# Layer norm 1 of batch 2 on x transposed by the host, and Q of unit 8 one block later

## The chip, the cores and the metric

The kernel runs on one core of one Trainium2 chip. The metric is the device time of one execution, in microseconds (us); lower is better. A core has a matrix engine (PE, with its weight loads shown apart as PEld), a vector engine (DVE), an activation engine (ACT), a general engine (POOL) and a sync engine (SP) that in this kernel issues nearly all transfers. Each engine takes its instructions strictly in the order in which the program lists them; semaphores hold an instruction until its inputs are there. DMA transfers issued by SP leave SP's queue in order too, and a transfer that has to wait holds all that stand behind it.

## The reference, cut to what matters

Four batches of a cross-attention block in float32: 512 rows of x, 512 rows of context, width 512, 16 heads of 32.

```python
x = layer_norm(hidden_states, ln1_w, ln1_b)
q = (x @ q_w + q_b).reshape(B, LQ, H, HD).transpose(0, 2, 1, 3)
k = (encoder_hidden_states @ k_w + k_b)...   # and v likewise
scores = jnp.einsum('bhqd,bhkd->bhqk', q, k) * scale
attn = jax.nn.softmax(jnp.where(mask, scores, mask_value), axis=-1)
out = jnp.einsum('bhqk,bhkd->bhqd', attn, v) @ cproj_w + cproj_b   # heads joined first
hidden = out + hidden_states
y = layer_norm(hidden, ln2_w, ln2_b)
y = jax.nn.gelu(y @ fc_w + fc_b, approximate=True) @ proj_w + proj_b
return hidden + y
```

Layer norm 1 is `(x - mu) * rsqrt(var + 1e-5) * w + b` over each row of x. The matrix products that follow contract over the width, so its result is wanted with the width on the partitions, that is transposed.

## The kernel before, in words

**Units, blocks, pairs.** The attention is cut into 16 units `w = 0..15`: batch `w // 4`, a group of four heads. Each unit is run in two halves of 256 query rows, which gives 32 blocks `p = 2w + half`, one after the other. In a block PE computes the scores (L317). DVE adds the mask and finds the row minimum (L323), ACT takes the exponential (L327), DVE transposes 32x32 squares into the tile `tb` (L335), and `copies` (L385 to L399) brings these into a tile with the keys on the partitions: four copies on POOL (L393) and twelve transfers issued by SP (L398). `attend` then multiplies by V (PE, L415) and scales by the reciprocal sums into `oT` (DVE, L420).

**When a pair is attended.** The result of a block is called a pair with the block's number. Around the change, from block 10 on, pair p - 2 is attended at the start of block p, ahead of the scores of that block. Pairs 8, 9, 10, 11 and so on use the one tile `pT`, so the copies and transfers of a pair are issued, in program order, right behind the `attend` of the pair before it. So POOL's copies of pair 10 stand in POOL's order behind all that block 10 gave to POOL, and ahead of what the fills of block 11 give to it; PE needs them for `attend` of pair 10, at the start of block 12.

**The rest of the work is written into the blocks by hand.** `put(p, ...)` lists work for block p as (cost, function). `block` runs the list in three stretches, `fill(0)` to `fill(2)`; in the first two it stops at a budget of 3.4. The costs only decide in which stretch an item is issued; within a block the items keep the list's order. `A(w)` gives the projections K, Q and V of unit w: `prep_k` (PE L255, ACT L257), `prep_q` (PE L267, ACT L268), `prep_v` (PE L278, ACT copy L283, then a bias on POOL, L309). `C(b)` is the output projection of a batch (PE L455, DVE L456). `stat`, `rs`, `norm` and `turns2` are layer norm 2: DVE statistics (L129, L130), POOL L135 to L148 for the reciprocal root (`ln_rs`), the normalisation of the four row tiles (`ln_norm`: ACT L153, for batch 0 the last of the four on DVE L157), and 16 transposes on PE (L166) with weight and bias applied on the way out of PSUM (ACT L171, DVE L169). `fc_sums` forms sums of the first MLP weights on POOL (L597, L600) and stores them (L689, L690); in block 10 it does two pairs of weight blocks. `fc_seven` (PE L646) is the first MLP product.

**Layer norm 1, two ways.** Batches 0 and 2 load x by rows, take statistics, normalise the four tiles and transpose them on PE: 16 transposes (L166) into four PSUM tiles and from there to `xT` with weight and bias. For batch 2 both the normalisation (L153) and the way out of PSUM (L171) are on ACT, since `(1, 2)` is in `BY_ACT` and `NORM_ACT`. Batches 1 and 3 (`BY_ROW`) also load x by rows for the statistics, but load x transposed by the host as well (`load_raw`). The two spreads, `rs` and `-mean*rs`, are turned by DVE (L203), stored to DRAM (`store_rn`, L206) and read back to all partitions (`load_rn`, L213). POOL multiplies and adds them in 128x512 tiles, eight instructions (`ln1_rows`, L218), and ACT applies weight and bias in four (`ln1_affine`, L222).

The blocks that the change edits read so before (line numbers of the profile are those of this kernel):

```python
put(9, c[:1], do(lambda: attend(3, 1)), x2[:2], c[1:2], x2[2:], stat(0, 0), c[2:3], stat(0, 1),
    c[3:], stat(0, 2), x3, stat(0, 3), rs(0))
k, q, v = A(8)
put(10, [k], norm(0, 0, 1), [v], norm(0, 2, 3), do(fc_sums), [q], t2)
k, q, v = A(9)
put(11, [k, v], some(2), pb_(0), mid=do(lambda: y_sums(0)))
```

Here `x2` holds the three parts of layer norm 1 of batch 2 (two of statistics, one of normalisation), `x3` its transposes, `t2` the transposes of layer norm 2 of batch 0, `some(2)` one first MLP product, `pb_(0)` four bias additions on POOL (L426).

Of the kernel before, what the change touches and what calls it, by code (L numbers as in the profile page):

```python
# [12 lines left out]
F32 = mybir.dt.float32  # L13
# [7 lines left out]
P = 128  # L21
B, L, D, H = 4, 512, 512, 16
# [3 lines left out]
ND = D // P  # L26
# [9 lines left out]
IN_G = (1, 3, 5, 7)  # L36
IN_XE = (25, 27, 29, 31)

BY_ROW = ((1, 1), (1, 3))
BY_ACT = ((1, 2),)  # L40
NORM_ACT = BY_ACT + ((2, 0), (2, 1))
MW = 8
WARM = 9
PW = 2 * NT * HG * HD
# [7 lines left out]
def xattn_block(ctx: ExitStack, tc: tile.TileContext, x, rawT, encT, mask, q_w, k_w, v_w, c_w, fc_w, p_w, vecs, rows, out):  # L52
# [3 lines left out]
    def pools(stack, **bufs):  # L56
        return [stack.enter_context(tc.tile_pool(name=n, bufs=k)) for n, k in bufs.items()]

    const, keep, hids, tiles, small = pools(ctx, const=1, keep=1, hids=4, tiles=4, small=4)
# [19 lines left out]
    eT, xT = (xe[:, i * ND * L : (i + 1) * ND * L].rearrange("p (d l) -> p d l", d=ND) for i in range(2))  # L79
# [35 lines left out]
    S = {"gelu": []}  # L115
# [3 lines left out]
    def acc_tile(name):  # L119
        n = count[5]  # L120
        count[5] += len(banks) > 1
        return banks[n // 4 % len(banks)].tile([P, D], F32, tag="acc", name=name)
# [9 lines left out]
    def ln_rs(key):  # L132

        ve = small.tile([P, NT], F32, tag="ve", name=f"ve{key[0]}_{key[1]}")
        nc.gpsimd.tensor_scalar(ve, S["mv", key][:, :, 1], EPS, 1.0, ALU.add, ALU.mult)  # L135
        if key in BY_ROW:
            rs, nm = rn[:, :NT], rn[:, NT : 2 * NT]
# [6 lines left out]
        S["rs", key] = rs  # L144
        if key in NORM_ACT:
            nm = small.tile([P, NT], F32, tag="nm", name=f"nm{key[0]}_{key[1]}")
# [4 lines left out]
    def ln_norm(key, t, dst, src):  # L151
        if key in NORM_ACT and (key, t) != ((2, 0), 3):
            nc.scalar.activation(  # L153
                dst, src, AF.Identity, bias=S["nm", key][:, t : t + 1], scale=S["rs", key][:, t : t + 1]
            )
            return
        nc.vector.tensor_scalar(  # L157
            dst, src, S["mv", key][:, t, 0:1], S["rs", key][:, t : t + 1], ALU.subtract, ALU.mult
        )

    def ln_turn(key, d, xn, dst):

        w, bi = (LN1W, LN1B) if key[0] == 1 else (LN2W, LN2B)
        tp = acc_tile(f"tp{key[0]}_{key[1]}_{d}")
        for t in range(NT):
            nc.tensor.transpose(tp[:, ts(t, P)], xn[t][:, ts(d, P)], ident)  # L166
        wd, bd = vec[:, w + d : w + d + 1], vec[:, bi + d : bi + d + 1]
        if d in (1, 2) and key not in BY_ACT:
            nc.vector.tensor_scalar(dst[:, d, :], tp, wd, bd, ALU.mult, ALU.add)  # L169
        else:  # L170
            nc.scalar.activation(dst[:, d, :], tp, AF.Identity, bias=bd, scale=wd)  # L171
# [23 lines left out]
            ln_rs((1, b))  # L195

    def load_raw(b):
        S["xn", b] = [tiles.tile([P, L], F32, tag="xn", name=f"raw_{b}_{d}") for d in range(ND)]
        for d in range(ND):
            nc.sync.dma_start(out=S["xn", b][d], in_=rawT[b, ts(d, P), :])  # L200

    def store_rn(b):
        nc.vector.transpose(rnT, rn)  # L203
        d = S["rn", b] = dram.tile([2, L], F32, tag=f"rn{b}", name=f"rn{b}")
        for i in range(NI):
            nc.sync.dma_start(  # L206
                out=d.rearrange("a (t i q) -> i (a t) q", i=NI, q=HD)[i], in_=rnT[i * HD : i * HD + 2 * NT, :]
            )

    def load_rn(b):  # L210
        S["rows", b] = [hids.tile([P, L], F32, tag="hid2", bufs=2, name=f"rn_{b}_{i}") for i in range(2)]
        for i in range(2):
            nc.sync.dma_start(out=S["rows", b][i], in_=S["rn", b][i : i + 1, :].broadcast_to([P, L]))  # L213

    def ln1_rows(b, *ds):
        for d in ds:
            for i, op in enumerate((ALU.mult, ALU.add)):
                nc.gpsimd.tensor_tensor(S["xn", b][d], S["xn", b][d], S["rows", b][i], op)  # L218

    def ln1_affine(b):  # L220
        for d in range(ND):
            nc.scalar.activation(  # L222
                xT[:, d, :], S["xn", b][d], AF.Identity,
                bias=vec[:, LN1B + d : LN1B + d + 1], scale=vec[:, LN1W + d : LN1W + d + 1],
            )
# [148 lines left out]
    def target(w, half):  # L374
        pair = 2 * w + half
        return "gt" if pair in IN_G else "xe" if pair in IN_XE else "pT"

    def exchange():

        while waiting and target(*waiting[0]) not in held:  # L380
            w, half = waiting.pop(0)
            held[target(w, half)] = w, half
            copies(w, half)
# [17 lines left out]
    def attend(w, half):  # L401

        b, g = divmod(w, NG)
        if g == 0 and half == 0:
            S["oT", b] = one.tile([P, NG, L], F32, tag="oT", name=f"oT_{b}")
        v, pT = S["v", w], S["pT", w, half]
        av = acc_tile(f"av_{w}_{half}")
        o = S["oT", b][:, g, ts(half, 2 * P)]
        shape, kw = "p (a i q) -> p a i q", dict(a=2, i=NI)
        pv = pT[:, :, :PW].rearrange("p i (a t h q) -> p t h a i q", a=2, t=NT, h=HG)  # L410
        p = [[pv[:, t, h] for h in range(HG)] for t in range(NT)]
        r = pT[:, :, PW:].rearrange("p i (a q) -> p a i q", a=2)
        for t in range(NT):
            for h in range(HG):
                nc.tensor.matmul(  # L415
                    av[ts(h, HD), : 2 * P].rearrange(shape, **kw), v[:, t, ts(h, HD)], p[t][h],
                    start=(t == 0), stop=(t == NT - 1),
                )
        o, a = o.rearrange(shape, **kw), av[:, : 2 * P].rearrange(shape, **kw)
        nc.vector.tensor_tensor(o, a, r, ALU.mult)  # L420
        del held[target(w, half)]
        exchange()
# [173 lines left out]
    def sub(o, x0, x1, engine=None):  # L596
        (engine or nc.vector).tensor_tensor(o, x0, x1, ALU.subtract)  # L597
# [19 lines left out]
    def y_sums(b):  # L617
        y11, y12, y21, y22 = y_blocks(b)
        e = nc.gpsimd if b == SPLIT else nc.vector
        sub(ys[:, 0], y12, y11)  # L620
        sub(ys[:, 1], y22, ys[:, 0])
        sub(y12, y22, y12, e)
        sub(ys[:, 2], y21, ys[:, 1], e)
# [55 lines left out]
    def fc_sums():  # L679

        while count[3] < len(fc_pairs) and count[3] < count[4] + 2:
            b, c = fc_pairs[count[3]]
            if ("fcw", b, 2 * c + 1) not in S:
                return
            x, y = raw_pair(b, c)
            s = wsum[:, count[3] % 2]
            a_sums(x[:, :2], x[:, 2:], y[:, :2], y[:, 2:], s[:, 0], s[:, 1], y[:, :2], s[:, 2], nc.gpsimd)
            if b == 0:
                nc.gpsimd.dma_start(out=sums_dram[c, :, :3], in_=s)  # L689
                nc.gpsimd.dma_start(out=sums_dram[c, :, 3], in_=y[:, :2])  # L690
            S["ws", b, c] = s[:, 0], s[:, 1], y[:, :2], s[:, 2]
            count[3] += 1
# [276 lines left out]
    def do(fn):  # L969
        return [(0.0, fn)]  # L970
# [4 lines left out]
    def A(w):  # L975
        if w >= NW:
            return []
        return [
            (CHAIN, lambda: prep_k(w)),
            (CHAIN, lambda: prep_q(w)),  # L980
            (CHAIN, lambda: prep_v(w)),
        ]
# [69 lines left out]
    def some(n):  # L1052
        taken = []
        while n > 0:
            n -= 1 if mlp[0][0] == CHAIN else 2
            taken.append(mlp.pop(0))
        assert n == 0
        return taken
# [10 lines left out]
    def pb_(b):  # L1069
        return do(lambda: proj_bias(b))  # L1070

    def rs(b):
        return do(lambda: ln_rs((2, b)))

    def stat(b, *ts_):
        return do(lambda: [stat2(b, t) for t in ts_])

    def norm(b, *ts_):
        return do(lambda: [norm2(b, t) for t in ts_])
# [3 lines left out]
    def put(p, *work, before=(), mid=()):  # L1083

        work = [item for part in work for item in part]
        ahead[p], mids[p] = list(before), list(mid)
        fills[p] = work
# [13 lines left out]
    x1, x2, x3, x4 = inputs(2)  # L1101
    k, q, v = A(7)
    c, t2 = C(0), turns2(0)
    put(7, [v6, k], cb(0))
    put(8, x1, [q, v], x4)
    put(9, c[:1], do(lambda: attend(3, 1)), x2[:2], c[1:2], x2[2:], stat(0, 0), c[2:3], stat(0, 1),
        c[3:], stat(0, 2), x3, stat(0, 3), rs(0))
    k, q, v = A(8)
    put(10, [k], norm(0, 0, 1), [v], norm(0, 2, 3), do(fc_sums), [q], t2)
    k, q, v = A(9)  # L1110
    put(11, [k, v], some(2), pb_(0), mid=do(lambda: y_sums(0)))

    x1, x2, x3, x4 = inputs(3)
    put(12, [q], some(2))
    k, q, v = A(10)
# [5 lines left out]
    k, q, v = A(11)  # L1121
    put(16, do(lambda: ln1_rows(3, *range(ND))), [k, q], some(2), h_(1, 0, 1))
    put(17, next_(lambda: ln1_affine(3)), h_(1, 2, 3), x4, cb(1), C(1))
    k, q, v = A(12)
    put(18, [q], some(2), [k])
    k, q, v = A(13)
# [3 lines left out]
    k, q, v = A(14)  # L1130
    t2 = turns2(1)
    put(22, [k, q], norm(1, 0, 1), some(2), norm(1, 2, 3))
    k15, q15, _ = A(15)
    put(23, some(1), [k15], t2, pb_(1), some(1), h_(2, 2, 3, 0, 1))
    c = C(2)
# [32 lines left out]
    c = cproj_last()  # L1168
# [59 lines left out]
```

## Time and profile before

| What | Value |
|---|---|
| median of 3 runs | 763.28 us (763.26 to 763.47) |
| profiled execution, its own time | 766.39 us |
| its span, first to last instruction | 764.3 us |
| mean granted PE clock | 0.997 of full |
| busy: PE, DVE, ACT, POOL | 757.5, 602.0, 337.1, 334.7 us |

The span is the stretch from the first to the last instruction of the profiled execution; 2.1 us of its own time lie around the span, and that own time is 3.1 us over the median of the three runs. In the rows shown below the first number of a timeline or chain row is the start in us from the start of the span, the second the duration; "x16" is a count of instructions merged in one row; a bracket gives the idle time of the engine ahead of the row and what ended it.

### The profile page before, as it was taken

The page shows a single profiled execution, that of the slowest core. Times are in us where ns is not written, and L with a number is a line of the kernel's source. Part 1 is how long each engine was busy: PE and PEld are TensorE (multiplying, and loading weights), DVE is VectorE, ACT ScalarE, POOL GpSimd, SP SyncE. Part 2 cuts the span into 40 slices and gives each one's busy share as a digit, 9 for nine tenths or more (in the row PEclk, how much of TensorE's full clock was granted, in tenths as well). Part 3 has the DMA queues.
Part 4 walks back from the last instruction along what each step waited for, and adds up shares of the span by engine and source line. Part 5 has one row for each costly group of instructions (what it writes and reads, how often), then busy time and mean ns, then how long its engine had stood idle before and what let it go on. Part 6 is the DMA issues. An engine that isn't in the chain of part 4 may idle for free.

```text
span 764.3 us, 12899 instructions
## 1 busy us (share of the span) xinstructions
PE 757.5 (99%) x4370; PEld 518.7 (68%) x4370; DVE 602.0 (79%) x1198; ACT 337.1 (44%) x766; POOL 334.7 (44%) x350
## 2 busy tenths in 40 slices
PE   9999999999989999999999999999999999999998
PEld 6655555566565545475464566458888899988997
DVE  3888999879976777887888889958877886747762
ACT  2566766565863475647753467501202221021200
POOL 1539447368653883443584444532060004303152
PEclk9999999999999999999999999999999999999999
DMA  8999889467796686765666867776724402146001
GB/s 325 341 255 243 204 207 254 111 199 196 214 251 212 194 242 169 184 184 130 167 141 179 212 194 197 171 226 212 270 97 131 163 31 90 36 133 218 1 15 42
DMA packets 60577, 134.59 MB, mean 176 GB/s; under 512 B 11312, under 2 KB 17072, under 8 KB 60384
## 3 DMA queue, kind: packets, MB, share of 16 engines
q1 hardware_dynamic: 58448, 126.73, 58.0%
q0 software_dynamic: 1920, 7.01, 2.8%
q8 instruction: 35, 0.57, 0.3%
q14 instruction: 30, 0.25, 0.1%
q10 hardware_dynamic: 144, 0.02, 0.0%
HBM read 69.23 MB, written 11.02 MB: 105 GB/s over the span
## 4 chain that ended last, share of the span: by engine, by line
PE 98%; SPq 1%; DMA 1%; issue 0%; DVE 0%; POOL 0%; POOLq 0%; DVEq 0%
PE q L646 25%; PE accp L705 11%; PE r L790 8%; PE sc L317 8%; PE av L415 8%; PE acck L255 7%; PE accq L267 7%; PE accc L455 6%; PE accv L278 5%; PE accv L298 3%; PE q1p L844 2%; PE q4p L826 2%; PE tp L166 1%; SPq L398 1%; DMA ptt<-q_w_dram 1%; PE warm L1023 1%
## 5 line engine op out<-in xcount | busy, mean ns | idle before, releaser
L327 ACT ACTIVATE ptt<-ptt,mn 128x512 f32<-128x512 f32 x256 | 181.7, 711 | 147.6 <-DVE mn L323 147.6
L323 DVE CUSTOM_DVE_ANT_0 ptt<-sc,mb 128x512 f32<-128x512 f32 x256 | 160.6, 682 | 20.1 <-PE sc L317 20.0
L335 DVE STREAM_TRANSPOSE tb<-ptt 128x1024 f32<-128x1024 f32 x128 | 153.3, 1217 | 1.0 <-ACT ptt L327 1.0
L393 POOL COPY pT<-tb 32x1088 f32<-32x1088 f32 x96 | 104.5, 1089 | 86.4 <-DMA pbt<-p_w_dram 28.0
L705 PE MATMUL accp<-pbt,gt 128*128 128x512 f32 x192 | 85.3, 596 | 0.0
L646 PE MATMUL q<-yT,gt 128*128 128x256 f32 x320 | 78.9, 380 | 0.0
L667 ACT ACTIVATE ga<-ga,vec 128x512 f32<-128x512 f32 x40 | 26.7, 714 | 93.3 <-DVE ga L600 83.5
L646 PEld LDWEIGHTS q<-yT,gt 128*128 128x128 f32 x320 | 61.0, 191 | 8.1
L705 PEld LDWEIGHTS accp<-pbt,gt 128*128 128x128 f32 x192 | 35.9, 190 | 44.6 <-issue 39.2
L317 PE MATMUL sc<-pbt 32*128 32x512 f32 x512 | 66.1, 621 | 0.0
L646 PE MATMUL q<-ys,gt 128*128 128x256 f32 x240 | 61.6, 380 | 0.0
L255 PE MATMUL acck<-xe,ptt 128*128 128x512 f32 x128 | 58.8, 603 | 0.2 <-issue 0.2
L267 PE MATMUL accq<-xe,ptt 128*128 128x512 f32 (+1 forms) x136 | 58.5, 575 | 0.0
L646 PEld LDWEIGHTS q<-ys,gt 128*128 128x128 f32 x240 | 45.7, 191 | 6.1
L600 DVE TENSOR_TENSOR ga<-q,ga 128x512 f32<-128x512 f32 (+1 forms) x60 | 36.2, 603 | 16.9 <-PE q L646 14.3
L415 PE MATMUL av<-pT,v 128*32 128x256 f32 x768 | 47.3, 387 | 2.0 <-DMA ptt<-q_w_dram 2.0
L327 ACT ACTIVATION_READ_ACCUMULATOR ptt<-ptt,mn 128x1 f32 x256 | 47.8, 187 | 0.0
L267 PEld LDWEIGHTS accq<-xe,ptt 128*128 128x128 f32 x136 | 24.9, 190 | 31.4 <-issue 23.0
L317 PEld LDWEIGHTS sc<-pbt 32*128 32x128 f32 x512 | 27.5, 187 | 26.0 <-issue 17.2
L255 PEld LDWEIGHTS acck<-xe,ptt 128*128 128x128 f32 x128 | 23.6, 192 | 31.2 <-issue 21.9
L455 PE MATMUL accc<-wc,oT 128*128 128x512 f32 x96 | 42.5, 598 | 0.0
L415 PEld LDWEIGHTS av<-pT,v 128*32 128x32 f32 x768 | 23.0, 111 | 26.2 <-issue 10.4
(219 smaller groups left out, 1265.4 us busy)
## 6 DMA issues: line engine op xcount, KB each, us to landing
pT<-tb SPq DMA_DIRECT2D x288, 136.0 KB, 2.4
pbt<-p_w_dram SPq DMA_DIRECT2D x40, 256.0 KB, 3.3
gt<-ws SPq DMA_DIRECT2D x20, 512.0 KB, 3.4
gt<-tb SPq DMA_DIRECT2D x48, 136.0 KB, 3.8
xe<-tb SPq DMA_DIRECT2D x48, 136.0 KB, 2.5
pbt<-fc_w_dram SPq DMA_DIRECT2D x24, 256.0 KB, 4.0
gt<-fc_w_dram SPq DMA_DIRECT2D x20, 256.0 KB, 3.2
ptt<-k_w_dram SPq DMA_DIRECT2D x16, 256.0 KB, 3.7
```

The lines of the kernel that those rows point to most:

```text
L255: nc.tensor.matmul(acc, S["wk", w][:, d, :], eT[:, d, :], start=(d == 0), stop=(d == ND - 1))
L267: nc.tensor.matmul(acc, S["wq", w][:, d, :], xT[:, d, c], start=(d == 0), stop=(d == ND - 1))
L317: nc.tensor.matmul(S["sc", w, qt][h], qT[r, ts(qt, P)], kT[r, :], start=True, stop=True)
L323: nc.vector.tensor_tensor_reduce(out=s, in0=S["sc", w, qt][h], in1=S["mb", w // NG], scale=1.0, scalar=FMAX, op0=ALU.add, op1=ALU.min, acc ...
L327: nc.scalar.activation(s, s, AF.Exp, bias=mn, scale=-1.0, accum_out=S["sums", w][:, qt, h : h + 1])
L335: nc.vector.transpose(tv[:, qt % 2, 2 * k : 2 * k + 2], S["ps", w, qt, k])
L393: nc.gpsimd.tensor_copy(pT[ts(i, HD), i], tb[ts(i, HD), i])
L415: nc.tensor.matmul(av[ts(h, HD), : 2 * P].rearrange(shape, **kw), v[:, t, ts(h, HD)], p[t][h], start=(t == 0), stop=(t == NT - 1),)
L455: nc.tensor.matmul(acc, S["oT", b][:, g, ts(t, P)], wc[:, g, :], start=(g == 0), stop=(g == NG - 1))
L646: nc.tensor.matmul(o, x[:, k], y[:, k], start=(k == 0), stop=(k == 1))
L705: nc.tensor.matmul(acc, gT[q % 2][:, k, ts(t, P)], S["pw", b, q * FQ + k], start=(k == 0), stop=(k == FQ - 1))
L790: nc.tensor.matmul(r, x[:, c], w[:, c], start=(c == 0), stop=(c == NP // 2 - 1))
```

## The change

Batch 2 joins `BY_ROW` and leaves `BY_ACT` (which goes). Its four normalisations on ACT, its 16 transposes on PE and their four ACT instructions go. In their place come, in block 9, four loads of transposed x, straight into `xT`, the turn of the spreads on DVE, four small stores and two loads that spread the rows; in block 10, eight POOL instructions behind the two pairs of `fc_sums`; in block 11, four ACT instructions. Q of unit 8, which reads `xT`, moves from ahead of `t2` in block 10 to the end of block 11, with its bias on ACT (L268) and the load of a later Q weight that it issues. The loads of x by rows and the statistics stay.

```diff
-BY_ROW = ((1, 1), (1, 3))
-BY_ACT = ((1, 2),)
-NORM_ACT = BY_ACT + ((2, 0), (2, 1))
+BY_ROW = ((1, 1), (1, 2), (1, 3))
+NORM_ACT = ((2, 0), (2, 1))
...
-        if d in (1, 2) and key not in BY_ACT:
+        if d in (1, 2):
...
     def load_raw(b):
-        S["xn", b] = [tiles.tile([P, L], F32, tag="xn", name=f"raw_{b}_{d}") for d in range(ND)]
+        S["xn", b] = [
+            xT[:, d, :] if b == 2 else tiles.tile([P, L], F32, tag="xn", name=f"raw_{b}_{d}") for d in range(ND)
+        ]
...
-    put(9, c[:1], do(lambda: attend(3, 1)), x2[:2], c[1:2], x2[2:], stat(0, 0), c[2:3], stat(0, 1),
-        c[3:], stat(0, 2), x3, stat(0, 3), rs(0))
-    k, q, v = A(8)
-    put(10, [k], norm(0, 0, 1), [v], norm(0, 2, 3), do(fc_sums), [q], t2)
+    put(9, c[:1], do(lambda: attend(3, 1)), x2[:2], do(lambda: load_raw(2)), c[1:2], do(lambda: store_rn(2)), stat(0, 0),
+        c[2:3], stat(0, 1), do(lambda: load_rn(2)), c[3:], stat(0, 2, 3), rs(0))
+    k, q8, v = A(8)
+    put(10, [k], norm(0, 0, 1), [v], norm(0, 2, 3), do(lambda: (fc_sums(), ln1_rows(2, *range(ND)))), t2)
     k, q, v = A(9)
-    put(11, [k, v], some(2), pb_(0), mid=do(lambda: y_sums(0)))
+    put(11, [k, v], some(2), pb_(0), do(lambda: ln1_affine(2)), [q8], mid=do(lambda: y_sums(0)))
```

## The prediction

> **What bounds the kernel now.** I read the page first, then the chain of waits around blocks 9 to 12, then ACT and POOL there in order of time.
>
> ```profile
> PE 757.5 (99%) x4370; PEld 518.7 (68%) x4370; DVE 602.0 (79%) x1198; ACT 337.1 (44%) x766; POOL 334.7 (44%) x350
> ...
> PE 98%; SPq 1%; DMA 1%; issue 0%; DVE 0%; POOL 0%; POOLq 0%; DVEq 0%
> ```
>
> PE is busy for 99% of the span and 98% of the chain that ended last lies on it. So PE work that is removed shortens the kernel, one for one, as long as no wait takes its place; and every wait put into PE lengthens it one for one. The chain where the change lies, with start and duration:
>
> ```profile
> 142.58 1.75 PE tp L166 x16
> 144.33 1.86 PE av L415 x32
> 146.19 1.93 PE sc L317 x16
> 148.12 3.63 PE acck L255 x8
> 151.75 3.57 PE accv L278 x32
> 155.33 3.44 PE accq L267 x8
> 158.76 0.22 PE tp L166 x2
> 158.98 0.01 issue
> 158.99 1.75 PE tp L166 x14
> 160.74 1.86 PE av L415 x32
> ...
> 171.74 6.04 PE q L646 x28
> 177.78 1.86 PE av L415 x32
> ```
>
> The reader is to see four things. The first row is the transposes that go. At 146.19 the scores of block 10 begin; K, V and Q of unit 8 follow, and then the transposes of layer norm 2 of batch 0 (158.76). The pair of transposes, then 0.01 us of issue, then fourteen: PE came there at the very moment at which their input did. And `attend` of pair 10 stands at 177.78, after block 11's K, V and first MLP product.
>
> **The transposes removed: -1.75 us.** Sixteen instructions, 1.75 us on the chain, with nothing beside them. Block 10 begins 1.75 us earlier, at 144.44, if nothing else there was waited for; DVE, ACT and POOL of block 10 follow its scores and move with it. The eight ACT instructions that go too are taken at nothing: ACT waits for DVE again in block 10 (the 1.59 us below), so their time is not asked for.
>
> **Q of unit 8 moved: +3.44 us, and nothing back.** Q leaves block 10 and comes back whole in block 11, the same work on PE. But it was the cover of a wait:
>
> ```profile
> 153.95 0.72 ACT L327 ACTIVATE ptt<-ptt,mn 128x512 f32<-128x512 f32 x1 [1.59 <-DVE mn L323]
> ...
> 155.38 0.66 ACT L257 ACTIVATE pbt<-acck,vec 128x512 f32<-128x512 f32 x1
> 155.94 1.51 ACT L153 ACTIVATE xn<-h,nm,rs 128x512 f32<-128x512 f32 x2
> 157.35 0.39 ACT L356 COPY rr<-rsum 128x256 f32<-128x256 f32 x1
> 157.65 0.58 ACT L283 COPY v<-accv 128x512 f32<-128x512 f32 x1
> 158.12 0.82 ACT L153 ACTIVATE xn<-h,nm,rs 128x512 f32<-128x512 f32 x1
> ```
>
> The normalised tiles that the transposes read come from ACT: two at 155.94, the third at 158.12, ready at 158.94, which is where PE's fourteen begin. ACT's own queue sets this: the last exponentials of block 10 wait for DVE, and then K's bias, two normalisations, the reciprocals, V's copy and the third normalisation run without a gap. None of it hangs on Q, whose bias on ACT comes after. So with block 10 1.75 us earlier the third tile is there at 157.19, and the transposes end 1.75 us earlier, at 158.99. PE, without Q, is at them at 158.76 - 1.75 - 3.44 = 153.57, and stands idle for 157.24 - 153.57 - 0.22 = 3.45 us, in two or three pieces. The Q that used to fill this then costs 3.44 us in block 11. By PE and ACT alone, `attend` of pair 10 would be reached at 177.78 - 1.75 + 3.44 = 179.47, that is 1.69 us later than before.
>
> **The eight POOL instructions: they become the last to arrive.** Before `attend` of pair 10, POOL must copy pair 10 into `pT`.
>
> ```profile
> 81.44 4.47 POOL L393 COPY pT<-tb 32x1088 f32<-32x1088 f32 x4
> ...
> 158.37 1.41 POOL L309 TENSOR_TENSOR v<-v,row 128x512 f32<-128x512 f32 x1 [6.91 <-ACT v L283]
> ...
> 169.05 4.69 POOL L393 COPY pT<-tb 32x1088 f32<-32x1088 f32 x4
> ...
> 253.49 10.38 POOL L218 TENSOR_TENSOR raw<-raw,rn 128x512 f32<-128x512 f32 x8
> ```
>
> V's bias starts when ACT has copied V; the weight sums and their stores run to 169.05; the copies end at 173.74, and PE takes them at 177.78: 4.04 us in hand. After the change the eight instructions of `ln1_rows` stand between the stores and the copies, in POOL's order. The same eight for batch 3, in one piece, took 10.38 us. POOL's start hangs on ACT's copy of V in block 10, so it moves with block 10: 158.37 - 1.75 = 156.62. Then 10.68 us to the end of the stores (169.05 - 158.37), 10.38 and 4.69: the copies end at 182.37. PE is there at 179.47 at the earliest, so it waits again, and `attend` of pair 10 begins at about 182.3 instead of 177.78. I take **+4.5 us**. The bounds of this step are narrow, since every part is a measured row: with the four copies at 4.47 us, as at 81.44, it is 0.2 less; if POOL's eight run beside DVE's sums of block 11 and are slowed by them, as an estimate some tenths more.
>
> The sum is not 1.69 + 4.5: the two waits lie one behind the other on PE, and POOL's chain runs past the first. From the start of block 10's scores to `attend` of pair 10 PE needs 31.6 us of work, as before; POOL's chain needs 38 us; and the block starts 1.75 us earlier. That is -1.75 + 38.0 - 31.6, some 4.6, the same figure from the other side. Behind that point nothing gives the time back: K, V and the MLP products follow on PE without gaps, so a shift there lasts to the end.
>
> **What I cost at nothing, and its cover.**
>
> ```profile
> 128.11 9.67 SPq L398 DMA_DIRECT2D pT<-tb  x12
> ...
> 240.51 1.30 SPq L206 DMA_DIRECT2D rn<-rnT  x4
> 242.73 0.82 SPq L213 DMA_DIRECT2D rn<-rn  x2
> ...
> L222 ACT ACTIVATE xe<-raw,vec x8: 797/804/817, 80.0 to 276.6; 128x512 f32<-128x512 f32 x8
> ```
>
> SP is through with pair 8 at 137.78. The loads of transposed x go out behind it (`xT` has no reader left: Q of unit 7 was in block 8), then the stores, which wait for DVE's turn of the spreads (one small instruction amid block 9's statistics), then the two spreading loads. For batch 3 stores to last load took 243.55 - 240.51 = 3.0 us, so SP is held to about 144, and what is queued behind it is the transfers of pair 9. These wait for `attend` of pair 8 anyway, which now ends at 144.4. If SP were held 2 us longer, pair 9 would still be in time for 158.99. The rows themselves are wanted by POOL only at about 167. The four ACT instructions (804 ns each) follow POOL's pairs one by one; the last ends near 178.5, and Q's fourth step on PE comes at about 178.6. Should it be late, it is late inside a stretch in which PE waits for POOL anyway. Behind them on ACT stand only Q's bias and the exponentials of block 12. The load that Q issues is held on SP until Q has run, with pair 11's transfers behind it, and those wait for `attend` of pair 10, which is later still. None of this can gain either.
>
> **The clock after a wait.** The one long wait in the trace of before has a price beside itself:
>
> ```profile
> 218.20:220.17 1.97, 0.00 (x1) 0.03 (x2) 1.76 (x3) 1.94 (x4) 0.00 (x0) 1.00 0.89 275
> 220.17:222.94 2.77, 2.77 (x36) 1.41 (x36) 0.04 (x1) 0.77 (x1) 0.00 (x0) 0.67 1.01 359
> 222.94:225.67 2.73, 2.73 (x17) 1.07 (x17) 1.26 (x4) 0.10 (x1) 2.10 (x2) 0.71 0.94 310
> ```
>
> PE idle for 1.97 us; then the granted clock is 0.67 and 0.71 over the next 5.5 us, and `attend` and the scores take 5.50 us in place of the 1.86 + 1.93 of the other blocks: 1.7 us lost. So the 3.45 us in block 10 will very likely drop the clock too. That costs nothing in the sum: PE would come to pair 10 at 181.2 instead of 179.47, still ahead of POOL at 182.3. What it decides is how long PE then waits: 1.1 us, which I take as too little for a second drop, or 2.8 us if the clock held, which is enough for one by the row above.
>
> The Trainium skill, in "TensorE: Matmul & The Clock Gate", Part 1, has the clock fall back to half only after an idle window of about 3.4 us. This trace contradicts that, with a drop after 1.97 us. By the page no second drop would come in either case, and the time would be that of the forecast; by the row the second drop is a rival.
>
> **The forecast.** Against the profiled execution: 766.39 + 4.5 = 770.9, span 768.8. The runs are compared without a profile, where the median is 763.28; a shift in PE's order is the same in both. Forecast **767.8 us**.
>
> **Rivals.**
> - A second clock drop at pair 10: 4.5 + 1.7 = +6.2, 769.5 us. For it, the drop after 1.97 us; against it, that the first wait will have slowed PE already, so that little is left to wait.
> - The clock drop at 220 goes away, because the later start meets another phase of whatever sets it: +4.5 - 1.7 = +2.8, 766.1 us. Against it: the three runs lie within 0.21 us of each other, so that drop is steady.
> - POOL does not decide: only the wait for the normalised tiles is left, +1.7, or +3.4 with its clock drop, 765.0 to 766.7 us. This needs POOL's chain shorter by 2.9 us (or 1.1): against it stands the 10.38 row.
> - Faster: both waits are absorbed and only the transposes count, -1.75, 761.5 us. It takes ACT, relieved of eight instructions, to bring the third tile 3.45 us earlier, and POOL's copies to end by 176.0 instead of 182.3. It decides from the point where ACT starts K's bias at 151.9, not 153.6. Against it: ACT had 1.59 us idle in block 10, waiting for DVE.
> - No change: the change does less than it says on PE, or part of each of the above cancels; nothing in the profile names such a case.
>
> **How the numbers follow.** Forecast 0.50, second drop 0.20, drop at 220 gone 0.12, POOL not deciding 0.08, faster 0.06, within the bound 0.04. A measurement of this kernel can tell about 0.2% (1.5 us) from no change. The case of +1.7 alone sits at that edge, so 0.01 of it goes to no change: faster 0.06, same 0.05, slower 0.89. The range goes from the wait of block 10 alone (765.0) to the second drop and some tenths of POOL's collisions (769.9).
>
> **What would show it.** Right: in block 10 PE idle for some 3.4 us ahead of the transposes, released by ACT L153; the granted clock below 1 behind it; POOL's copies of pair 10 ending about 38 us after the start of block 10's scores; PE's `attend` waiting for POOL L393; block 12 on shifted by a constant. Wrong: no idle time ahead of the transposes (then ACT was not what they waited for), `attend` of pair 10 released by something else than POOL, or a shift that shrinks after block 12.

## The result, and the profile after

The changed kernel took 771.00 us (median of 4 runs, 768.99 to 774.32) against 763.27 us for the kernel before (4 runs, 761.89 to 763.47): a ratio of 1.0108 [1.0085, 1.0130], slower by about 7.7 us. The forecast was 767.8 us with a range up to 769.9. The direction was right, the size was not: 4.5 us were forecast, and the range ended 1.1 us short.

The profiled execution of the changed kernel has its own time at 774.32 us. From its page: the busy times, and the chain that ended last by engine. Line numbers of the changed kernel are one higher than those of the kernel before from L200 on, and one lower ahead of it.

```profile
PE 760.1 (98%) x4354; PEld 518.4 (67%) x4354; DVE 604.5 (78%) x1199; ACT 334.4 (43%) x762; POOL 345.1 (45%) x358
...
PE 93%; DVE 4%; ACT 1%; issue 1%; DMA 1%; POOL 0%; DVEq 0%; POOLq 0%
```

PE runs 16 instructions fewer and is busy for 2.6 us *longer*. Of the chain 5% have passed from PE to DVE, ACT and issue. POOL, which the forecast had as the last to arrive, has 0%. The waits of PE say who came last instead; columns are total us, times, longest:

```profile
PE accq L268 <- ACT xe L223: 2.7, 1, 2.7
PE tp L165 <- ACT xn L152: 2.6, 3, 1.2
PE av L416 <- DMA ptt<-q_w_dram: 2.6, 1, 2.6
```

The second row is the forecast wait for the normalised tiles. The first is the moved Q itself: it waits for the last of the four new ACT instructions. The third is the transfer ahead of pair 13, which the profile of before had too (218 to 220) and which is spoken of below. PE in order of time:

```profile
154.83 0.33 PE L165 MATMUL tp<-ident,xn 128*128 128x128 f32 x1 [1.11 <-ACT xn L152]
155.54 0.33 PE L165 MATMUL tp<-ident,xn 128*128 128x128 f32 x1 [0.38 <-ACT xn L152]
157.03 3.25 PE L165 MATMUL tp<-ident,xn 128*128 128x128 f32 x14 [1.16 <-ACT xn L152]
...
179.99 5.40 PE L268 MATMUL accq<-xe,ptt 128*128 128x512 f32 x8 [2.67 <-ACT xe L223]
185.32 1.93 PE L416 MATMUL av<-pT,v 128*32 128x256 f32 x32
...
228.43 3.59 PE L416 MATMUL av<-pT,v 128*32 128x256 f32 x32 [2.64 <-DMA ptt<-q_w_dram]
```

Both waits have a slow stretch behind them. The fourteen transposes take 3.25 us instead of 1.75, and Q takes 5.40 instead of 3.44 (in the chain, whose rows do not overlap; in a timeline an undisturbed Q has 3.60 to 3.70 us). The windows over these stretches have the granted clock in the last column but two:

```profile
157.00:159.00 2.00, 1.97 (x9) 1.98 (x10) 0.39 (x1) 0.78 (x1) 1.92 (x3) 0.50 0.32 117
159.00:161.00 2.00, 2.00 (x22) 1.38 (x25) 1.23 (x2) 0.69 (x1) 1.73 (x3) 0.68 0.00 0
...
180.00:183.00 3.00, 3.00 (x5) 1.37 (x6) 1.81 (x3) 2.05 (x3) 2.84 (x4) 0.63 0.00 0
183.00:186.00 3.00, 3.00 (x19) 1.14 (x21) 0.00 (x0) 0.57 (x1) 3.00 (x3) 0.80 0.02 5
```

So the terms up to `attend` of pair 10 are: transposes -1.75; slow transposes 3.25 - 1.75 = +1.50; Q +3.44; the wait ahead of Q +2.67; slow Q 5.40 - 3.44 = +1.96. The sum is +7.82. The trace has the same: from `attend` of pair 7, where nothing is changed yet (130.15 before, 129.93 after), to `attend` of pair 10 (177.71 before, 185.32 after) it is 47.56 us before and 55.39 after, +7.83 us. Pair 14 and those behind it stand a constant 8.28 to 8.29 us later than before: 7.83, less the 0.22 by which pair 7 was earlier, and 0.67 more at pair 13, where the wait is longer than before.

Why ACT was late with Q's input is told by the chain of waits between block 11's scores and Q:

```profile
165.77 0.62 DVE ys L598
...
166.48 2.13 DVE ys L598
168.60 1.68 DVE yT L598
170.28 1.67 DVE ys L598
171.96 0.60 DVE ptt L324
...
176.09 1.52 ACT ptt L328 x4
...
178.47 0.48 ACT v L284
...
179.23 0.72 ACT xe L223
...
179.99 5.40 PE accq L268 x8
```

The first four rows are `y_sums(0)`, sums of the transposed activations that DVE forms amid block 11's mask-and-minimum work (L597 before, L598 after; neither is edited). Behind them wait the other four row minima, behind these ACT's exponentials, and behind those, in ACT's queue, V's copy among others and at last the new `ln1_affine` (L223). DVE in order of time, before:

```profile
166.14 0.92 DVE L597 TENSOR_TENSOR ys<-yT 128x512 f32<-128x512 f32 x1
167.17 1.03 DVE L597 TENSOR_TENSOR ys<-yT,ys 128x512 f32<-128x512 f32 x1
168.12 0.68 DVE L597 TENSOR_TENSOR yT<-yT 128x512 f32<-128x512 f32 x1
168.73 0.68 DVE L597 TENSOR_TENSOR ys<-yT,ys 128x512 f32<-128x512 f32 x1
```

and in the changed kernel, DVE and then POOL:

```profile
165.69 0.69 DVE L598 TENSOR_TENSOR ys<-yT 128x512 f32<-128x512 f32 x1
166.48 2.13 DVE L598 TENSOR_TENSOR ys<-yT,ys 128x512 f32<-128x512 f32 x1
168.53 1.75 DVE L598 TENSOR_TENSOR yT<-yT 128x512 f32<-128x512 f32 x1
170.21 1.75 DVE L598 TENSOR_TENSOR ys<-yT,ys 128x512 f32<-128x512 f32 x1
```

```profile
166.77 11.49 POOL L219 TENSOR_TENSOR xe<-xe,rn 128x512 f32<-128x512 f32 x8
178.20 4.47 POOL L394 COPY pT<-tb 32x1088 f32<-32x1088 f32 x4
```

The four sums took 3.31 us before and 6.32 after. The three long ones lie beside POOL's eight row instructions. POOL's copies end at 182.67; that is close to the forecast 182.37, but PE comes only at 185.32, so they hold nobody.

### The profile page after: what moved, and what is told of

Read it like the earlier page. It is cut to its first block, busy times and chain, and to the rows that moved or that the text cites. A ratio compares the mean times of both kernels' runs of the same rounds, so it can differ in the third digit from the quotient of the medians.

```text
span 772.5 us, 12886 instructions
## 1 busy us (share of the span) xinstructions
PE 760.1 (98%) x4354; PEld 518.4 (67%) x4354; DVE 604.5 (78%) x1199; ACT 334.4 (43%) x762; POOL 345.1 (45%) x358
## 4 chain that ended last, share of the span: by engine, by line
PE 93%; DVE 4%; ACT 1%; issue 1%; DMA 1%; POOL 0%; DVEq 0%; POOLq 0%
PE q L647 24%; PE accp L706 11%; PE r L791 8%; PE sc L318 8%; PE accq L268 8%; PE av L416 7%; PE acck L256 6%; PE accv L279 4%; PE accc L456 4%; PE accv L299 3%; PE q1p L845 2%; PE q4p L827 2%; DVE ptt L324 1%; PE tp L165 1%; DVE tb L336 1%
## 5 line engine op out<-in xcount | busy, mean ns | idle before, releaser
L268 PE MATMUL accq<-xe,ptt 128*128 128x512 f32 (+1 forms) x136 | 60.2, 589 | 2.7 <-ACT xe L223 2.7
L268 PEld LDWEIGHTS accq<-xe,ptt 128*128 128x128 f32 x136 | 25.5, 194 | 35.5 <-issue 23.7
```

What stands on the lines that cost most here:

```text
L268: nc.tensor.matmul(acc, S["wq", w][:, d, :], xT[:, d, c], start=(d == 0), stop=(d == ND - 1))
```

## The experiments

Theory: the wait for the normalised tiles slows the clock and delays block 11; DVE's four sums then fall beside the POOL row instructions and take twice as long; through ACT's queue that makes Q wait, and the clock drops again. The rival is the forecast: POOL's copies of pair 10 decide. A second rival is that the rows are late themselves, so that ACT waits for POOL. A third is that Q's move alone makes up the loss. Since executions differ ahead of the change already (`attend` of pair 7 stands between 128.67 and 132.13 us), shifts are counted from that `attend` to the one of pair 10, against the 47.56 us of before. The first four columns of numbers come from one profiled execution of each kernel, the ratio from all its runs.

| Kernel | sums on DVE, us | wait ahead of Q | Q | shift to pair 10 | ratio to the kernel before |
|---|---|---|---|---|---|
| changed kernel | 6.32 | 2.67 | 5.40 | +7.83 | 1.0108 [1.0085, 1.0130] |
| the same again | 6.31 | 2.66 | 5.40 | +7.81 | 1.0107 [1.0075, 1.0139] |
| Q's move alone | 4.53 | none | 3.60 | +5.05 | 1.0065 [1.0043, 1.0086] |
| rows early | 4.69 | 1.03 | 3.70 | +5.74 | 1.0046 [1.0025, 1.0068] |
| V of unit 9 as cover | 4.57 | 4.01 | 5.40 | +6.19 | 1.0098 [1.0065, 1.0130] |
| no rows | 4.53 | 0.87 | 3.70 | +4.27 | 1.0058 [1.0034, 1.0082] |
| rows that only write | 2.74 | none | 3.60 | +3.30 | 1.0038 [1.0019, 1.0056] |
| PE held busy | 4.83 | 1.18 | 3.70 | +4.87 | 1.0057 [1.0036, 1.0079] |
| both repairs | 3.66 | none | 3.60 | -1.62 | 1.0007 [0.9987, 1.0026] |
| both, and margin | 3.65 | none | 3.60 | -1.62 | 0.9985 [0.9969, 1.0001] |

One regularity of the table carries the theory. In the five profiles in which block 11 has all its PE work and Q waits (changed kernel, the same again, rows early, no rows, PE held busy), the wait is the time of DVE's sums less 3.65 or 3.66 us, whether and wherever POOL's rows stand.

### Q's move alone

```diff
 (kernel before)
-put(10, [k], norm(0, 0, 1), [v], norm(0, 2, 3), do(fc_sums), [q], t2)
+put(10, [k], norm(0, 0, 1), [v], norm(0, 2, 3), do(fc_sums), t2)
-put(11, [k, v], some(2), pb_(0), mid=do(lambda: y_sums(0)))
+put(11, [k, v], some(2), pb_(0), [q8], mid=do(lambda: y_sums(0)))
```

> The kernel before with one edit: Q of unit 8 goes to the end of block 11; layer norm 1 of batch 2 stays as it was. If the lost cover in block 10 costs what the forecast says: PE idle some 3.4 us ahead of the transposes of layer norm 2, then a slow clock for one stretch (the profile of the changed kernel shows the fourteen transposes at 3.25 us in place of 1.75), attend of pair 10 late by 3.4 to 5 us, 766.7 to 768.4 us. If the wait were absorbed: 763.3. No POOL row work, so DVE's sums of block 11 take some 3.2 us as before.

Measured: 768.35 us (10 runs, 766.48 to 770.81). PE:

```profile
158.16 0.33 PE L166 MATMUL tp<-ident,xn 128*128 128x128 f32 x1 [1.47 <-ACT xn L153]
158.86 0.33 PE L166 MATMUL tp<-ident,xn 128*128 128x128 f32 x1 [0.38 <-ACT xn L153]
160.35 3.17 PE L166 MATMUL tp<-ident,xn 128*128 128x128 f32 x14 [1.16 <-ACT xn L153]
163.45 2.13 PE L415 MATMUL av<-pT,v 128*32 128x256 f32 x32
```

DVE's sums take 4.53 us here, beside POOL's copies, and not the 3.2 that were expected; but Q waits for nothing, since its input was ready a block earlier. There is no row of layer norm 1 on POOL, and the waits and the slow transposes are there all the same. The shift of +5.05 is Q's 3.44, plus 3.17 - 1.75 = 1.42 and 2.13 - 1.93 = 0.20 of slow clock. So Q was the cover, and the loss behind an uncovered wait is its slow tail. But it doesn't make up the whole of the 7.83 us, in which the removed transposes have already saved 1.75: the rest of the change adds 7.83 + 1.75 - 5.05 = 4.5 us.

### The rows early

```diff
 (changed kernel)
-put(10, [k], norm(0, 0, 1), [v], norm(0, 2, 3), do(lambda: (fc_sums(), ln1_rows(2, *range(ND)))), t2)
+put(10, [k], norm(0, 0, 1), do(lambda: ln1_rows(2, *range(ND))), [v], norm(0, 2, 3), do(fc_sums), t2)
```

> The changed kernel with POOL's eight row instructions ahead of V's bias and the weight sums of block 10, where POOL waited. Collision theory (row instructions beside DVE's sums slow DVE by 3 us, which makes the exponentials of block 11, ACT's four affine instructions and Q late): the sums take some 3.2 us instead of 6.2, Q waits for nothing, attend of pair 10 moves against before by -1.75 + 3.44 + up to 1.5 of slow clock, 765.0 to 766.6 us. Forecast's theory (POOL's copies of pair 10 are last): the copies end near 176.8, so the same time, but with the copies the last to arrive in the changed kernel. If neither holds, and the load of all POOL work counts: near 771.

Measured: 767.16 us (12 runs, 765.25 to 770.23).

```profile
151.27 10.52 POOL L219 TENSOR_TENSOR xe<-xe,rn 128x512 f32<-128x512 f32 x8
```

```profile
179.55 3.70 PE L268 MATMUL accq<-xe,ptt 128*128 128x512 f32 x8 [1.03 <-ACT xe L223]
```

The rows are now done before block 11, but DVE's sums lie beside POOL's weight sums (128x256) instead: 1.24, 1.03, 1.21 and 1.21 us, so they do not fall to the expected 3.2 us. The wait ahead of Q falls from 2.67 to 1.03 us and Q runs at full clock. It still waits, although POOL has been done with the rows since 161.8 us and Q starts at 179.55: ACT's queue decides, not POOL. The profiled execution is the slowest of the twelve; its shift of +5.74 is 2 us more than the median is. Of it 2.76 us are slow clock in block 10, which here reaches into `attend` of pair 9 (3.19 instead of 1.93 us); behind it stands a wait of 2.42 us at pair 13. Which of the two the shorter executions lack was not seen.

### Without the rows

The eight POOL instructions are left out: x goes into Q without its mean and its spread taken out. The weight and bias on ACT stay.

```diff
 (changed kernel)
-put(10, [k], norm(0, 0, 1), [v], norm(0, 2, 3), do(lambda: (fc_sums(), ln1_rows(2, *range(ND)))), t2)
+put(10, [k], norm(0, 0, 1), [v], norm(0, 2, 3), do(fc_sums), t2)
```

> The changed kernel without POOL's eight row instructions (x enters Q without mean and spread). Left is the move of Q and the transposes gone. Collision and POOL theories alike: DVE's sums take some 3.2 us, Q waits for nothing, attend of pair 10 at -1.75 + 3.44 + up to 1.5, 765.0 to 766.6 us. What is left against the changed kernel (771.0) is the price of the rows, 4.4 to 6 us; if the loads and stores of x and the spreads cost something, it stays near 769.

Measured: 767.45 us (12 runs, 766.03 to 774.56). Without POOL's 10 us, POOL is idle ahead of V's bias and cannot be last, yet the kernel is some 4 us slower than before. DVE and POOL:

```profile
167.02 1.58 DVE L598 TENSOR_TENSOR yT<-yT 128x512 f32<-128x512 f32 x1
168.52 1.57 DVE L598 TENSOR_TENSOR ys<-yT,ys 128x512 f32<-128x512 f32 x1
```

```profile
166.75 5.43 POOL L394 COPY pT<-tb 32x1088 f32<-32x1088 f32 x4
```

POOL's copies of pair 10 have moved up and now take the rows' place beside the sums; they are slowed themselves, 5.43 instead of 4.47 us. So leaving the rows out does not take the collision away, and the expectation of undisturbed sums and no wait failed. The wait of 0.87 us ahead of Q goes with sums of 4.53 us.

### Rows that only write

The eight POOL instructions are kept in number, place and output, but each fills its tile with a constant and reads nothing; Q is computed from that constant.

```diff
 (changed kernel)
-nc.gpsimd.tensor_tensor(S["xn", b][d], S["xn", b][d], S["rows", b][i], op)
+if b == 2:
+    nc.gpsimd.memset(S["xn", b][d], float(i))
+else:
+    nc.gpsimd.tensor_tensor(S["xn", b][d], S["xn", b][d], S["rows", b][i], op)
```

> The changed kernel with POOL's eight row instructions of batch 2 replaced by eight that only write the same 128x512 tiles (constants; x does not enter Q). If two engines that read collide: DVE's sums of block 11 run at some 0.7 us each while POOL writes, some 3 us in all. If any POOL instruction beside them slows them: 1.3 us and more each as in the changed kernel. POOL's instructions are likely shorter, so the copies of pair 10 come earlier and the time is near that of the kernel without rows, 766 to 767.5 us in either case; what is read is the four durations.

Measured: 765.63 us (10 runs, 763.81 to 767.36).

```profile
165.60 0.69 DVE L601 TENSOR_TENSOR ys<-yT 128x512 f32<-128x512 f32 x1
166.40 0.69 DVE L601 TENSOR_TENSOR ys<-yT,ys 128x512 f32<-128x512 f32 x1
167.00 0.68 DVE L601 TENSOR_TENSOR yT<-yT 128x512 f32<-128x512 f32 x1
167.61 0.68 DVE L601 TENSOR_TENSOR ys<-yT,ys 128x512 f32<-128x512 f32 x1
```

```profile
166.54 4.27 POOL L220 MEMSET xe<- 128x512 f32 x8
```

The last three sums run beside POOL's instructions as in the changed kernel, at 0.68 to 0.69 us each, like the first, which is ahead of them: an undisturbed sum costs that. There is no wait ahead of Q, and the shift of +3.30 is PE's own terms alone: -1.75, +3.44 and 1.6 of slow clock behind the wait in block 10 (fourteen transposes 2.54, `attend` 2.76). So of the changed kernel's +7.83 the rows' reads and their longer run on POOL (11.49 instead of 4.27 us), and what both set off, make up 4.5; this run does not part the two. What slowed DVE, though, was not that POOL was busy, but that it read. The Trainium skill, "SBUF — State Buffer", section "Who interferes with whom", says just that: a DVE instruction with two inputs in SBUF contends with a GpSimd instruction that reads SBUF, and not with one that only writes. The runs agree: 0.68 us beside writes, 1.57 beside POOL's copies, 1.75 to 2.18 beside its two-input 128x512 instructions.

### PE held busy in the idle stretch

```diff
 (changed kernel)
+def spin(n):                  # products of the identity with itself, read by nobody
+    t = acc_tile("spin")
+    for _ in range(n):
+        nc.tensor.matmul(t[:, :P], ident, ident, start=True, stop=True)
...
-put(10, ..., do(lambda: (fc_sums(), ln1_rows(2, *range(ND)))), t2)
+put(10, ..., do(lambda: (fc_sums(), ln1_rows(2, *range(ND)))), [(0.6, lambda: spin(14))], t2)
```

> The changed kernel with 14 matrix products of the identity on PE (some 3.1 us, their result is not read) between V of unit 8 and the transposes of layer norm 2, where PE stood idle. If the clock drop behind that wait is part of the cost: the fourteen transposes take 1.5 us instead of 3.25, block 11 starts 1.5 us earlier, DVE's sums start ahead of POOL's rows and take 3.2 to 4 us instead of 6.2, Q waits for less, and pair 10 is attended when POOL's copies end, near 182: 767.5 to 768.5 us against 771.0. If the forecast was right that a slow clock there costs nothing because POOL is last: 771.

Measured: 767.51 us (7 runs, 765.89 to 768.01), mean granted clock 1.000. PE:

```profile
156.93 2.09 PE L165 MATMUL tp<-ident,xn 128*128 128x128 f32 x16
...
177.24 3.70 PE L268 MATMUL accq<-xe,ptt 128*128 128x512 f32 x8 [1.18 <-ACT xe L223]
182.60 1.93 PE L416 MATMUL av<-pT,v 128*32 128x256 f32 x32 [1.66 <-POOL pT L394]
```

The 14 products are 28 instructions in the trace and fill 3.29 us. This is the forecast's case: the clock holds, `attend` of pair 9 starts 1.5 us earlier as counted from pair 7, only the last of DVE's sums meets the rows (2.18 us), Q waits 1.18 us, and `attend` of pair 10 waits for POOL. The shift is +4.87 where +4.5 was forecast; by the medians of these runs it is 767.51 - 762.34 = 5.2 us. So the clock drop in block 10 is what turned the forecast's case into the measured one, and 14 products that nobody reads bring 7.83 - 4.87 = 3.0 us back in the trace.

### V of unit 9 as the cover

V of unit 9 goes from block 11 into block 10, ahead of the transposes, in the place that Q had. Its result lies in the free ends of two tiles, since its own has a reader until later.

```diff
 (changed kernel)
-put(10, ..., do(lambda: (fc_sums(), ln1_rows(2, *range(ND)))), t2)
+put(10, ..., do(lambda: (fc_sums(), ln1_rows(2, *range(ND)))), [v9], t2)
-put(11, [k, v], some(2), pb_(0), do(lambda: ln1_affine(2)), [q8], mid=do(lambda: y_sums(0)))
+put(11, [k], some(2), pb_(0), do(lambda: ln1_affine(2)), [q8], mid=do(lambda: y_sums(0)))
```

> The changed kernel with V of unit 9 moved from block 11 to block 10, between V of unit 8 and the transposes (its tile lies in two free ends of larger tiles). It gives back 3.6 us of cover and leaves POOL's rows where they are. Cover: no idle time and no slow clock ahead of the transposes. Then block 11 starts 1.75 us earlier than before, DVE's sums lie ahead of the rows and take some 3.2 us (collision theory), and PE comes to Q early and waits for ACT's affine instructions, which now wait for POOL; attend of pair 10 waits for POOL's copies, which end near 183.7: +6, 769 to 771 us. If cover were all: 761.5.

Measured: 771.23 us (6 runs, 767.50 to 773.57); the profiled execution is the fastest of the six.

```profile
156.39 1.91 PE L166 MATMUL tp<-ident,xn 128*128 128x128 f32 x16
...
175.78 5.40 PE L269 MATMUL accq<-xe,ptt 128*128 128x512 f32 x8 [4.01 <-ACT xe L224]
182.94 1.93 PE L420 MATMUL av<-pT,v 128*32 128x256 f32 x32 [1.76 <-POOL pT L398]
```

The wait in block 10 is gone and the transposes run at full clock. But block 11 has 3.6 us of PE work less, so PE is at Q earlier, and waits there for 4.01 us; behind that the clock is slow again (granted 0.56 from 175.8 to 178.8 us), and then POOL's copies are waited for. Covering the one wait alone only moves it: there is no more work to put ahead of Q than there was.

### Both repairs

The cover of V of unit 9, the rows early, one pair of `fc_sums` in place of two in block 10, and the four ACT instructions already at the end of block 10, so that Q can go ahead of the first MLP product.

```diff
 (on the kernel with V of unit 9 as the cover)
-put(10, [k], norm(0, 0, 1), [v], norm(0, 2, 3), do(lambda: (fc_sums(), ln1_rows(2, *range(ND)))), [v9], t2)
+put(10, [k], norm(0, 0, 1), do(lambda: ln1_rows(2, *range(ND))), [v], norm(0, 2, 3), do(lambda: fc_sums(1)), [v9], t2,
+    do(lambda: ln1_affine(2)))
-put(11, [k], some(2), pb_(0), do(lambda: ln1_affine(2)), [q8], mid=do(lambda: y_sums(0)))
+put(11, [k], [q8], some(2), pb_(0), mid=do(lambda: y_sums(0)))
```

> A version meant to keep the gain: the changed kernel with V of unit 9 as cover in block 10, POOL's rows ahead of V's bias, one pair of weight sums instead of two in block 10, ACT's four affine instructions at the end of block 10 (so ahead of the exponentials of block 11), and Q of unit 8 ahead of the first MLP product in block 11. If lost cover, the rows' place and ACT's order are all that the change cost: no PE wait in blocks 10 and 11, no slow clock there, only the transposes' 1.75 us count, 761.5 to 762.5 us against 763.4 of before. If the rows cost something by their mere load (DVE's sums beside POOL's work, transfers), 763 to 765.

Measured: 764.20 us (12 runs, 759.14 to 765.58), no difference from before, and not the 761.5 to 762.5 that were expected. PE:

```profile
178.07 1.93 PE L420 MATMUL av<-pT,v 128*32 128x256 f32 x32
...
220.82 1.93 PE L420 MATMUL av<-pT,v 128*32 128x256 f32 x32 [2.28 <-DMA ptt<-q_w_dram]
```

In blocks 10 and 11 PE no longer waits, and `attend` of pair 10 comes 1.62 us earlier than before, which is the transposes' 1.75. So the change itself is worth what its removed work is worth, where nothing new is waited for. Which of the four moves are needed was not separated. In this execution a transfer is then late by 2.28 us at pair 13 and takes it all back. Another 2 us of its 765.00 lie ahead of pair 7, where the kernels do the same (`attend` of pair 7 at 132.13 us, against 130.15 before): PE waits there for the first loads (0.31 and 0.88 us) and for DVE (1.00 us, at 54). What makes up the median of 764.20 is therefore not shown.

### Both repairs, and margin for the later transfer

```diff
 (on the kernel with both repairs)
-put(14, [q], some(2), x1)
-put(15, x2[:1], V(10), x2[1:2], ...
+put(14, [q], V(10), some(2), x1)
+put(15, x2[:1], x2[1:2], ...
```

> The version with cover and early rows, and besides V of units 10 and 11 moved from block 15 to block 14, which gives the transfers of pair 13 some 7 us more before PE attends it. In that version the gain of 1.6 us stood in blocks 10 and 11 and a wait of 2.3 us for pair 13 followed it at 218 us. If that wait is what takes the gain: none there, 760.5 to 761.5 us against 762.3 to 763.4 of before. If something else does: near 764 again.

Measured: 762.00 us (12 runs, 759.57 to 764.45) against 762.71 (17 runs, 760.65 to 766.44). The wait at pair 13 is down to 0.7 us in its profile, where none was expected, and the median is above the expected 760.5 to 761.5. This is the one version with a median below that of the kernel before, and its interval reaches 1: a gain of about 1 us that these runs do not make sure.

### Both kernels once more

> The kernel before once more, for a second trace. If the wait at 218 us and the slow clock behind it belong to every execution: there again, span near 764.3. If they come and go: span near 761, mean clock 1.000, no PE wait near 218.

> The changed kernel once more, for a second trace and more times. By the reading so far: PE idle some 2.7 us ahead of the transposes, released by ACT; the four sums on DVE 4.5 to 6.5 us; PE waits for ACT's affine instructions ahead of Q of unit 8, and the more so the longer the sums took (wait = sums - 3.6 us); median 769 to 772 us.

Measured: a second profiled execution of the kernel before has its own time at 762.64 us, granted clock 1.000, and at pair 13 nothing is waited for:

```profile
218.15 1.93 PE L415 MATMUL av<-pT,v 128*32 128x256 f32 x32
```

The changed kernel took 770.48 us (6 runs): 768.61, 768.62, 768.78 and 772.18, 773.19, 773.23. The profile of the run at 768.61 has the same waits of 2.6 and 2.7 us in blocks 10 and 11 and the same slow Q, and none at pair 13. So the two waits belong to the change, and the one at pair 13 comes and goes in both kernels. Where it was there, the twelve transfer issues of pair 13 on SP had taken 8.5 to 9.2 us; where not, 7.7 to 8.2. What lengthens them stays open, and that it makes the spread between 768.6 and 773.2 is likely by its size (2.6 us and a slow stretch of 1.7) and not shown run by run.

## Why the prediction was wrong in size

**Right.** The transposes were worth 1.75 us: with everything else covered, the shift is -1.62. Q was the cover of a wait: the rows show 1.11, 0.38 and 1.16 us idle ahead of the transposes, released by ACT L152, with two lone transposes of 0.33 us between. That is 2.65 us, where 3.45 in pieces were forecast. The clock fell behind it. POOL's copies ended at 182.67, forecast 182.37; this is in part luck, since the rows took 1.1 us longer than forecast, while V's bias, the weight sums and the copies were 0.8 us ahead of it. SP and the transfers stayed off PE's path around the change, and the shift is constant later on.

**"That costs nothing in the sum."** This step on the clock drop of block 10 failed first, and with it the path: Q, and not POOL's copies, was the last that `attend` of pair 10 stood behind, which the prediction itself had named as a sign of being wrong. The drop cost 1.5 us in the transposes, and its cover was said to be the wait for POOL. But those 1.5 us also push block 11's scores, and DVE's sums behind them, into the time of POOL's rows. With the clock held, the wait ahead of Q was 1.18 instead of 2.67 us, and the forecast's sum nearly came out (+4.87, with POOL's copies as the last to arrive).

**"As an estimate some tenths more."** The collision of POOL and DVE was put on POOL, where it was 11.49 instead of 10.38 us. The larger part fell on DVE: 6.32 instead of 3.31 us, +3.0. This term was mis-sized by a factor of several, and it was looked for on the wrong engine. It takes both errors to make the result: with the drop but sums of 2.74 us (rows that only write) Q waits for nothing, and without the drop only the last sum meets the rows.

**"The four ACT instructions follow POOL's pairs one by one."** They do not: they stand in ACT's queue behind block 11's exponentials, which wait for DVE's row minima, which wait for the sums. In the changed kernel they begin at 179.12 us, when POOL has been through the rows for 0.9 us:

```profile
179.12 2.94 ACT L223 ACTIVATE xe<-xe,vec 128x512 f32<-128x512 f32 x4
```

The forecast counted what stands behind them on ACT and not what stands ahead. That Q would be "late inside a stretch in which PE waits for POOL anyway" was true of the start of Q alone, at 179.99: with its 3.44 us it would have ended at 183.4, 0.8 us past POOL's copies. At the slow clock it took 5.40 and ended at 185.39.

**The second drop.** It was a rival at 0.20 (+6.2 in all), placed at `attend` of pair 10. It came one step earlier, on Q: there it cost 5.40 - 3.44 = 1.96 us, where 1.7 had been put on `attend` and the scores.

**The baseline.** The drop at 220 of the profile of before was taken for steady, since three runs agree within 0.21 us, and the 3.1 us between the profiled execution and the median were put down to the profile. The second profile of before says otherwise: 762.64 us with a profile, near the median, and neither wait nor drop. The two profiled executions differ by 3.75 us, and the wait of 1.97 with its drop of 1.7 make up 3.7 of it. The forecast by differences did not suffer from this, but the rival that let this drop "go away" would have taken it off a median that did not hold it.

**A slip in a rival.** For the third tile to come 3.45 us earlier than forecast, ACT would have to start K's bias at 153.6 - 3.45 = 150.2 us; the 151.9 counts from the kernel before. In the changed kernel it started at 153.41.

## What to carry to other kernels

Before work is moved off an engine, ask which wait it covers, and charge the uncovered wait with a possible slow-clock tail and with what this tail pushes next to what: here 1.5 us of slow transposes put DVE beside POOL and cost several more. For an instruction that gets a new input, follow the in-order queue of the engine that makes that input from its front, not only what stands behind; and for work moved to POOL, ask which two-input DVE work runs at that time. A few products that nobody reads, put into an idle stretch of PE that can't be filled otherwise, were worth some 3 us here.

## What of the hardware was not expected

DVE's 128x512 sums with two inputs take 0.68 us alone or beside POOL's writes, 1.03 to 1.24 beside POOL's 128x256 sums, 1.57 beside its 32x1088 copies and up to 2.18 beside its 128x512 sums, while POOL's own eight row instructions go only from 10.38 to 11.49 us.

The clock does not follow from the length of one wait: it fell behind 1.97 us (before, at pair 13), 2.67 us (Q) and 2.64 us (pair 13 after), but not behind the 2.28 us at pair 13 with both repairs (`attend` behind it at 1.93 us, granted clock 1.00), nor behind 2.42 us there with the rows early:

```profile
226.07 1.93 PE L416 MATMUL av<-pT,v 128*32 128x256 f32 x32 [2.42 <-DMA ptt<-q_w_dram]
```

By the Trainium skill, "TensorE: Matmul & The Clock Gate", Part 1, the activity window of about 3.4 us runs freely and does not start anew with a kernel. If a drop depends on where in that window a wait falls, it can come behind one wait and not behind a longer one, as here; no run shows the window itself. That page also wants a whole idle window ahead of a drop. This does not fit, since the three waits with a drop are shorter.
